# Gate logits from normalized tokens and head outputs, in a perceiver layer with routed experts

## The chip, the core and the metric

The kernel runs on one core of a Trainium2 chip. The metric is device time in microseconds (us); the time before is the median of three runs. In the text PE is TensorE (matrix multiplication), DVE is VectorE, ACT is ScalarE, POOL is GpSimd and SP is SyncE, which here only issues transfers. One execution of the kernel was profiled, and every row that is shown comes from it unless another kernel is named. "Granted clock" is the share of full speed that PE's clock was given.

## What is computed

There are 32 sequences of 32 tokens, 512 wide, so 1024 tokens or eight tiles of 128. All numbers are float32. Three steps follow each other, each added to its input:

```
x = x + cross_attention(layernorm(x), context)    # context: 32 x 257 x 384
x = x + self_attention(layernorm(x))              # 16 heads of 32, rotary q and k
x = x + experts(layernorm(x))

def experts(xf):                                  # 8 experts, hidden 1024
    scores = sigmoid(xf @ gate_w.T + balance_bias)
    top2 = the two best experts of each token, shares normalized to 1
    h = silu(xf @ w1[e].T)
    return sum over the two: share * (h @ w2[e].T)
```

The change bears on the gate, `xf @ gate_w.T`. Its argument is the normalized sum of what went into self attention, x, and of what came out of it: `out @ Wo.T + bo`, where `out` holds the heads' outputs.

## The kernel before

The eight token tiles are treated as four pairs, numbered 0 to 3 (`p`); tile 2p + i is tile i of the pair. Cross attention runs first (in groups `g` of four sequences), and its last groups already hold the first steps of pair 0. Then comes a loop over pairs 0 to 2, written out by hand: it attends for pair p and prepares pair p+1 meanwhile. Pair 3 is written out after the loop, mixed with the first work of the experts. A scheduler sets each engine's order from this text, with fixed queues: an instruction that waits holds back all behind it on its engine.

The steps, with their names in the code and the PSUM or SBUF names that the profile shows:

- `norm` (and `normalized`, `rstd_of`, L180) normalizes a pair for self attention into y: statistics on DVE, the power -1/2 on POOL (rs, L185), scaling on ACT. `turn` transposes y into yT on PE (spt), with one copy on ACT and one on DVE (syT). `project` (pp, L380) makes q and k in halves, `rotate` (L396 to L409) turns them on DVE, `values` (ppv, L818) makes v.
- `scores` (pqs, L833) multiplies q and k of all heads in pieces of 32 by 32. It writes a PSUM tile of which there is one only, shared with `attend` (pos, L875). DVE takes the maximum and subtracts it (smx L841, sex L843), ACT makes the exponential (L849). `shares` sums, divides and transposes on DVE (ssm, src, sex, aT). `attend` multiplies with v, and DVE adds the value bias (oT, L882).
- `finish` multiplies oT by the output matrix (ppo, L894), adds the result to x on DVE (L898), and writes x out. `norm2` takes statistics of the new x and scales it (fy, L915).
- The gate comes one pair later. `gate_turn` transposes the raw x of a tile on PE (fpt, L931), ACT copies it (fyT, L933), and `gate_logits` multiplies it by the centred gate weights gwc (pg, L940), four multiplications with only 8 columns each. DVE scales with rs and adds the bias (lg, L944). Since gwc has its mean over the 512 inputs removed, the mean of x needs no subtraction.
- `pick` (L955 to L999) finds the two best experts and their shares by some 25 small DVE operations and an exponential on ACT (a sigmoid in the last pair). `places` (pr, L1010 to L1032) counts the rows ahead, and POOL scatters the rows with four indirect DMAs into lists in memory (xs_d), one list for each expert. These lists were filled with zeros by eight DMAs (`fill`, L169), which SP issues after the attention weights.
- `order` (L1053 to L1116) counts after pair 2, ranks the experts, and lets SP load the first weights (w1), the first two blocks of rows of the biggest expert (xse) and w2. `early_turn` (xpe), `early_hidden` (phe, L1148) and `early_out` (poe, L1162) compute this expert's early rows. All other rows follow in the expert stage.

PSUM tiles named ps rotate through four buffers. A column group is a multiplication with 32 stationary columns that writes 32 of the 128 partitions; four can stand side by side. The kernel already uses such groups in `xquery` (pbt, L467) and `xmix` (pc, L599).

The large room `ewp` (three buffers of 16 KB in each partition) serves context tiles, then pair 0's data (`rooms[0]`, `rooms[1]`), then expert weights.

## Time and profile before

| | |
|---|---|
| median of three runs | 565.48 us (563.83 to 568.45) |
| the profiled execution's own time | 566.19 us |
| its span in the trace | 564.5 us |
| mean granted PE clock | 0.975 |
| PE busy | 525.1 us, 93% of the span, 4716 records |
| PE weight loads busy | 340.8 us, 60% |
| DVE busy | 254.0 us, 45% |
| ACT busy | 123.2 us, 22% |
| POOL busy | 83.5 us, 15% |
| self attention, roughly | 140 to 302 us of the span |

The busy shares say how much of the span an engine had something in work. They do not say what a stage waits for. For that one reads the chain that ended last (for each piece: start, length, what), the timeline of an engine (start, length, engine, line, operation, output and inputs, shape, count, and in brackets the idle time before it and what ended it), and windows (busy time of each engine in a stretch, with the granted clock). A float32 multiplication appears as two records, a transpose as one.

### The profile page before, as it was taken

Reading aid. Unit: us, or ns where it says so; the run is one execution under the profiler, and the core shown is the slowest. Engines: PE = TensorE matmul, PEld = TensorE weight load, DVE = VectorE, ACT = ScalarE, POOL = GpSimd, SP = SyncE. Lnnn points to the kernel's source line nnn. Section 1 sums busy time; section 2 is a strip of 40 time slices with the busy share of each in tenths; the row PEclk is TensorE's granted clock in tenths of the full one; section 3 lists DMA queues with packets and bytes.
Section 4 is the critical chain, followed back from the end, with each engine's and each line's share of the span. In section 5 each row is a group of like instructions: output and inputs, shape, how many; then the busy total and the mean of one; then the engine's idle time right before and its main releaser. Section 6 shows DMA issues by size and latency. Waiting matters only on the chain.

```text
span 564.5 us, 11301 instructions
## 1 busy us (share of the span) xinstructions
PE 525.1 (93%) x4716; PEld 340.8 (60%) x4716; DVE 254.0 (45%) x758; ACT 123.2 (22%) x274; POOL 83.5 (15%) x120
## 2 busy tenths in 40 slices
PE   6999797999999999998969999999999999999992
PEld 3646354566584875776548456547657475768580
DVE  6657778747567765668534032203122121222220
ACT  3534444323313312212022021002011010102010
POOL 2110221110001012021302110122120202112211
PEclk9999999999999999798989999999999999999997
DMA  8999979999910002012295341657553554746421
GB/s 281 383 372 395 318 244 324 357 387 386 384 58 38 3 24 93 2 42 76 81 381 216 90 100 69 238 133 221 167 168 111 128 198 154 215 159 197 161 27 21
DMA packets 43086, 104.51 MB, mean 185 GB/s; under 512 B 3985, under 2 KB 7185, under 8 KB 42002
## 3 DMA queue, kind: packets, MB, share of 16 engines
q1 hardware_dynamic: 38434, 94.91, 46.8%
q0 software_dynamic: 4592, 8.78, 7.7%
q8 instruction: 39, 0.64, 0.5%
q14 instruction: 21, 0.17, 0.1%
HBM read 75.50 MB, written 28.18 MB: 184 GB/s over the span
## 4 chain that ended last, share of the span: by engine, by line
PE 69%; DVE 2%; issue 1%; ACT 1%; POOL 0%; POOLq 0%; ACTq 0%
PE ph L1344 18%; PE fpo L1397 15%; PE pp L380 8%; PE ppv L818 5%; PE ppo L894 4%; PE fpq L1311 4%; PE phe L1148 3%; PE poe L1162 2%; PE pg L940 2%; PE pos L875 2%; PE pqs L833 2%; PE phb L1365 1%; PE xpt L1326 1%; ACT xT L176 1%; PE fpt L931 1%
## 5 line engine op out<-in xcount | busy, mean ns | idle before, releaser
L1344 PE MATMUL ph<-xT,w 128*128 128x288 f32 (+4 forms) x448 | 100.2, 382 | 3.1 <-ACT xT L176 3.1
L1344 PEld LDWEIGHTS ph<-xT,w 128*128 128x128 f32 x448 | 79.0, 190 | 19.6 <-ACT xT L176 3.7
L1397 PE MATMUL fpo<-w,hT 128*128 128x512 f32 x192 | 84.4, 596 | 0.0
L1397 PEld LDWEIGHTS fpo<-w,hT 128*128 128x128 f32 x192 | 35.9, 190 | 43.9 <-issue 43.7
L1350 DVE TENSOR_TENSOR hT<-ph,sg 128x288 f32<-128x288 f32 (+4 forms) x56 | 23.6, 422 | 61.7 <-ACT sg L1349 61.7
L1402 DVE TENSOR_SCALAR fob<-fpo,share 128x512 f32<-128x512 f32 x12 | 9.0, 751 | 77.0 <-PE fpo L1397 77.0
L1349 ACT ACTIVATE sg<-ph 128x288 f32<-128x288 f32 (+4 forms) x56 | 21.5, 383 | 85.0 <-PE ph L1344 83.5
L505 DVE BATCH_NORM_STATS2 st<-n 128x6 f32<-128x384 f32 x64 | 32.7, 549 | 2.1 <-DMA n<-in_ctx_dram 2.1
L194 POOL DMA_INDIRECT out_dram<-fob,idx x12 | 18.5, 1542 | 93.7 <-DVE fob L1402 80.9
L176 ACT COPY xT<-xpt 128x512 f32<-128x512 f32 (+2 forms) x12 | 6.0, 496 | 112.5 <-PE xpt L1326 112.4
L894 PE MATMUL ppo<-ao,oT 128*128 128x512 f32 x64 | 30.1, 624 | 0.0
L194 POOL DMA_INDIRECT out_dram<-fob,plc x9 | 13.9, 1541 | 101.5 <-DVE fob L1316 84.9
L519 POOL TENSOR_TENSOR rs<-v,mhalf 128x9 f32<-128x9 f32 x8 | 14.4, 1798 | 80.7 <-DVE v L517 42.6
L380 PE MATMUL pp<-syT,aq 128*128 128x256 f32 x96 | 25.7, 427 | 0.0
L633 PE MATMUL po<-wvo,uT 128*128 128x512 f32 x48 | 22.4, 602 | 1.2 <-ACT uT L626 1.2
L818 PE MATMUL ppv<-av,syT 128*128 128x512 f32 x48 | 23.3, 635 | 0.0
L475 PE MATMUL pq<-x1T,mq 128*128 128x256 f32 x96 | 23.1, 385 | 0.0
L1311 PE MATMUL fpq<-w,hT 128*32 128x128 f32 (+1 forms) x576 | 22.3, 309 | 0.0
L380 PE MATMUL pp<-syT,ak 128*128 128x256 f32 x96 | 22.3, 385 | 0.0
L1032 POOL DMA_INDIRECT xs_d<-fy,pi x16 | 17.0, 1064 | 35.3 <-DVE pi L1028 21.9
L380 PEld LDWEIGHTS pp<-syT,aq 128*128 128x128 f32 x96 | 20.2, 216 | 3.3
L894 PEld LDWEIGHTS ppo<-ao,oT 128*128 128x128 f32 x64 | 12.6, 199 | 14.2 <-issue 14.0
(269 smaller groups left out, 732.5 us busy)
## 6 DMA issues: line engine op xcount, KB each, us to landing
xs_d<-zero SPq DMA_DIRECT2D x8, 2112.0 KB, 20.5
w<-in_w1T_dram SPq DMA_DIRECT2D x16, 1024.0 KB, 8.4
w<-in_w2T_dram SPq DMA_DIRECT2D x16, 1024.0 KB, 8.2
nT<-in_ctxT_dram SPq DMA_DIRECT2D x8, 1542.0 KB, 9.6
n<-in_ctx_dram SPq DMA_DIRECT2D x32, 384.0 KB, 7.0
xs<-xs_d SPq DMA_DIRECT2D x4, 528.0 KB, 9.3
x_sb<-in_x_dram SPq DMA_DIRECT2D x8, 256.0 KB, 6.7
out_dram<-x_sb SPq DMA_DIRECT2D x8, 256.0 KB, 2.0
```

What stands on the lines that cost most here:

```text
L194: nc.gpsimd.indirect_dma_start(out=dst, out_offset=bass.IndirectOffsetOnAxis(ap=place, axis=0), in_=ob, in_offset=None, bounds_check=n * ( ...
L380: nc.tensor.matmul(pp[:, i, :], w[:, k, ts(e, P)], yT[:, k, :], start=(k == 0), stop=(k == KD - 1),)
L475: nc.tensor.matmul(pq[:, 0 : 2 * P], mq[:, k, ts(c, P)], x1T[:, k, :], start=(k == 0), stop=(k == KD - 1),)
L505: nc.vector.bn_stats(st[:, r, :], n[:, r // 2, r % 2, :] if r < 8 else nl)
L633: nc.tensor.matmul(po, uT[:, c, :], wvo[:, c, :], start=(c == 0), stop=(c == KC - 1))
L818: nc.tensor.matmul(pp, st[p]["yT"][:, k, ts(i, P)], av[:, k, :], start=(k == 0), stop=(k == KD - 1),)
L894: nc.tensor.matmul(pp, st[p]["oT", i][:, k].rearrange("p b q -> p (b q)"), ao[:, k, :], start=(k == 0), stop=(k == KD - 1),)
L1311: nc.tensor.matmul(po[ts(g, Q), 0:w], hT[:, f, ts(h, Q)], w2[:, f, ts(j, w)], start=(f == 0), stop=(f == KF - 1),)
L1344: nc.tensor.matmul(ph[:, 0:n], w1[:, k, ts(f, P)], t["xT"][:, k, 0:n], start=(k == 0), stop=(k == KD - 1),)
L1349: nc.scalar.activation(sg[:, 0:n], ph[:, 0:n], AF.Sigmoid)
L1350: nc.vector.tensor_mul(hT[:, f, 0:n], ph[:, 0:n], sg[:, 0:n])
L1397: nc.tensor.matmul(po, hT[:, f, ts(c, P)], w2[:, f, :], start=(f == 0), stop=(f == KF - 1),)
```

## The change

Four things are changed together.

1. **The gate's logits are put together from two parts.** For the part of x before self attention, `gate_tokens` multiplies gwc with yT, the already transposed normalized tokens (pgy, four column groups, both tiles at once). `gate_scaled` adds the four groups by a multiplication with the matrix `summed` (pgt) and ACT multiplies by the standard deviation std that the normalization had divided by (ga). For the part from self attention, `gate_heads` multiplies oT with gwo, the product of the output matrix and the gate weights (pgh, column groups), and `gate_logits` adds the groups (pg) and both parts (DVE, then rs and bias as before). The transposes of x (fpt, fyT) are gone.
2. **gwo is made once in the kernel.** `gate_fold` multiplies gwc with the output matrix (pgf) and with its bias (pgb), `gate_fold2` adds groups and transposes (pgo). This needs the output matrix in its other orientation, so it is loaded a second time (o2, 1 MB), into the second half of `rooms[1]`, and the eight zero fills are issued behind this load. gwc is padded with zeros from 8 to 32 columns.
3. **Logits and `pick` of pairs 0 and 1 stand in their own pair's turn**, after the next pair's `values`, and not in the next pair's turn behind the second scores.
4. **The last pair and its early rows are ordered anew**: `values` of both tiles stand among the scores, `order` comes ahead of `attend`, a one-column sigmoid loads ACT's table early, both copies of the early rows' transposes are on ACT, and both tiles' logits come ahead of `early_turn`.

The core of the diff:

```diff
+                std = spool.tile([P, 2], F32, tag="std", name="std")
+                nc.vector.tensor_tensor(std, ve, rs, ALU.mult)
...
-                        fill(aw["last"])
...
+                if g == NTT - 2:
+                    with tc.issue_after(aw["last"]):
+                        room(0, "sw0")
+                        aw["o2"] = load_weight(aWo, rooms[1][:, 2 * KD * N2 :])
+                    fill(aw["last"])
...
+            def gate_fold():
+                pm = ps.tile([P, D], F32, tag="ps", name="pgf")
+                for k in range(KD):
+                    nc.tensor.matmul(
+                        pm[ts(k, Q), :], gwc[:, k, :], aw["o2"][:, k, :],
+                        start=True, stop=True,
+                    )
+                gf = rooms[1][:, 2 * KD * N2 : 2 * KD * N2 + D]
+                nc.scalar.copy(gf, pm)
...
+            def gate_fold2(gf):
+                pm = ps.tile([P, D], F32, tag="ps", name="pgo")
+                for k in range(KD):
+                    nc.tensor.matmul(
+                        pm[:, ts(k, Q)], gf[:, ts(k, P)], summed, start=True, stop=True
+                    )
...
-            def gate_turn(p, i):
-                pt = ps.tile([P, KD, P], F32, tag="ps", name="fpt")
-                for k in range(KD):
-                    nc.tensor.transpose(pt[:, k, :], x_sb[:, t, ts(k, P)], ident)
-                xT = rt.tile([P, KD, P], F32, tag="fyT", name="fyT")
-                nc.scalar.copy(xT, pt)
...
+            def gate_tokens(p):
+                pg = ps.tile([P, D], F32, tag="ps", name="pgy")
+                for k in range(KD):
+                    nc.tensor.matmul(
+                        pg[ts(k, Q), 0:N2], gwc[:, k, :], st[p]["yT"][:, k, :],
+                        start=True, stop=True,
+                    )
...
+            def gate_heads(p, tiles=(0, 1)):
+                for j, i in enumerate(tiles):
+                    oT = st[p]["oT", i]
+                    for k in range(KD):
+                        nc.tensor.matmul(
+                            pg[ts(k, Q), ts(j, P)], gwo[:, k, :],
+                            oT[:, k].rearrange("p b q -> p (b q)"),
+                            start=True, stop=True,
+                        )
...
-                    evac(c, xT[:, :, ts(c, P)], pt)
+                    nc.scalar.copy(xT[:, :, ts(c, P)], pt)
...
+            gf = gate_fold()
+            gate_tokens(0)
             for p in range(NP - 1):
                 scores(p, 0)
+                gate_tokens(p + 1)
+                if p == 0:
+                    gate_scaled(0)
+                    gate_fold2(gf)
                 project(p + 1, 0, 0)
                 shares(p, 0)
                 scores(p, 1)
-                if p:
-                    gate(p - 1, 0)
-                    gate(p - 1, 1)
-                    pick(p - 1)
+                gate_scaled(p + 1)
...
+                gate_heads(p)
                 finish(p, 0)
                 norm2(p, 0)
                 finish(p, 1)
                 norm2(p, 1)
                 if p < NP - 2:
                     values(p + 1)
+                    gate_logits(p)
+                    pick(p)
                     step(turn, p + 2)
             p = NP - 1
             scores(p, 0)
-            gate_turn(p - 1, 0)
-            gate_turn(p - 1, 1)
-            scores(p, 1)
-            gate_logits(p - 1, 0)
-            gate_logits(p - 1, 1)
+            values(p, (0,))
+            gate_logits(p - 1)
+            last = scores(p, 1)
             pick(p - 1)
-            values(p, (0,))
             shares(p, 0)
+            values(p, (1,))
+            with tc.issue_after(last.ins), tc.issue_after(st[p - 1]["en"]):
+                table = keep.tile([P, 1], F32, name="table")
+                nc.scalar.activation(table, mhalf[:, 0:1], AF.Sigmoid)
             places(p - 1)
+            order()
             attend(p, 0)
-            values(p, (1,))
-            order()
             shares(p, 1)
+            gate_heads(p, (0,))
             finish(p, 0)
-            norm2(p, 0)
-            attend(p, 1)
-            gate(p, 0)
+            with tc.issue_after(attend(p, 1).ins):
+                norm2(p, 0)
+            gate_heads(p, (1,))
             finish(p, 1)
             norm2(p, 1)
+            gate_logits(p)
             early_turn()
-            gate_turn(p, 1)
             early_hidden(0)
-            gate_logits(p, 1)
             pick(p)
```

More of the change, by code (lines that the diff above doesn't have):

```diff
@@ L43 @@
 ASCALE = HD ** -0.5
-G1, B1, BQ, BK, BV, AQ, AK, AV, NCOL = 0, 4, 8, 12, 16, 20, 24, 28, 44
+G1, B1, BQ, BK, BV, AQ, AK, AV, AO, NCOL = 0, 4, 8, 12, 16, 20, 24, 28, 32, 44
 RBO, RAO, RBB, NROW = 0, 512, 1024, 1032
@@ L69, in tile_perceiver_layer @@
     aWoT: bass.AP,
+    aWo: bass.AP,
     gateT: bass.AP,
@@ L185, in rstd_of @@
         nc.gpsimd.tensor_tensor(rs, ve, mhalf[:, :n], ALU.pow)
-        return rs
+        return rs, ve
     def stats_of(src, mv):
@@ L337, in normalized @@
                     stats_of(x_sb[:, 2 * p + i, :], mv[:, i, :])
-                rs = rstd_of(mv, 2)
+                rs, ve = rstd_of(mv, 2)
+                std = spool.tile([P, 2], F32, tag="std", name="std")
+                nc.vector.tensor_tensor(std, ve, rs, ALU.mult)
+                st[p]["std"] = std
                 nb = spool.tile([P, 2], F32, tag="nb", name="nb")
@@ L805, in tile_perceiver_layer @@
             nc.vector.tensor_scalar_mul(gm, pm[:, 0:NE], -1.0 / D)
-            gwc = keep.tile([P, KD, NE], F32, name="gwc")
+            gwc = rt.tile([P, KD, Q], F32, tag="gwc", bufs=1, name="gwc")
+            nc.gpsimd.memset(gwc, 0.0)
             nc.vector.tensor_tensor(
-                gwc, gw, gm.unsqueeze(1).to_broadcast([P, KD, NE]), ALU.add
+                gwc[:, :, 0:NE], gw, gm.unsqueeze(1).to_broadcast([P, KD, NE]), ALU.add
             )
+            summed = copies[:, 0, 0, :]
+            gwo = rt.tile([P, KD, Q], F32, tag="gwo", bufs=1, name="gwo")
+            bg = rt.tile([P, 1], F32, tag="bg", bufs=1, name="bg")
+            def gate_fold():
[7 more added lines that the diff above has]
+                nc.scalar.copy(gf, pm)
+                pm = ps.tile([P, D], F32, tag="ps", name="pgb")
+                for k in range(KD):
+                    nc.tensor.matmul(
+                        pm[ts(k, Q), 0:1], gwc[:, k, :], col[:, AO + k : AO + k + 1],
+                        start=True, stop=True,
+                    )
+                nc.scalar.copy(bg, pm[:, 0:1])
+                return gf
+            def gate_fold2(gf):
[4 more added lines that the diff above has]
+                    )
+                nc.scalar.copy(
+                    gwo, pm[:, 0 : KD * Q].rearrange("p (k q) -> p k q", q=Q)
+                )
             scatters = []
@@ L848, in scores @@
                 )
-                nc.scalar.activation(ex, ex, AF.Exp, scale=ASCALE)
                 st[p]["ex", i] = ex
+                return nc.scalar.activation(ex, ex, AF.Exp, scale=ASCALE)
             def shares(p, i):
@@ L881, in attend @@
                 oT = wk.tile([P, KD, 4, T], F32, tag="oT", bufs=3, name="oT")
-                nc.vector.tensor_tensor(
+                added = nc.vector.tensor_tensor(
                     oT.rearrange("p k b q -> p b k q"),
@@ L888, in attend @@
                 st[p]["oT", i] = oT
+                return added
             def finish(p, i):
@@ L909, in norm2 @@
                 stats_of(x_sb[:, t, :], mv[:, 0, :])
-                rs = rstd_of(mv, 1)
+                rs, _ = rstd_of(mv, 1)
                 nb = spool.tile([P, 1], F32, tag="nb1", name="nb")
@@ L920, in norm2 @@
                 st[p]["rs", i] = rs
-            def gate(p, i):
-                gate_turn(p, i)
-                gate_logits(p, i)
-            def gate_turn(p, i):
-                t = 2 * p + i
-                pt = ps.tile([P, KD, P], F32, tag="ps", name="fpt")
-                for k in range(KD):
-                    nc.tensor.transpose(pt[:, k, :], x_sb[:, t, ts(k, P)], ident)
-                xT = rt.tile([P, KD, P], F32, tag="fyT", name="fyT")
-                nc.scalar.copy(xT, pt)
-                st[p]["gT", i] = xT
@@ L936, in gate_logits @@
-            def gate_logits(p, i):
-                xT = st[p]["gT", i]
-                pg = ps.tile([P, D], F32, tag="ps", name="pg")
+            def gate_tokens(p):
+                pg = ps.tile([P, D], F32, tag="ps", name="pgy")
                 for k in range(KD):
                     nc.tensor.matmul(
-                        pg[:, 0:NE], xT[:, k, :], gwc[:, k, :],
-                        start=(k == 0), stop=(k == KD - 1),
-                    )
-                nc.vector.scalar_tensor_tensor(
-                    st[p]["lg"][:, i, :], pg[:, 0:NE], st[p]["rs", i], bb,
-                    op0=ALU.mult, op1=ALU.add,
-                )
+                        pg[ts(k, Q), 0:N2], gwc[:, k, :], st[p]["yT"][:, k, :],
+                        start=True, stop=True,
+                    )
+                gy = rt.tile([P, N2], F32, tag="gy", name="gy")
+                nc.scalar.copy(gy, pg[:, 0:N2])
+                st[p]["gy"] = gy
@@ new lines, in gate_scaled @@
+            def gate_scaled(p):
+                pg = ps.tile([P, D], F32, tag="ps", name="pgt")
+                for i in range(2):
+                    nc.tensor.matmul(
+                        pg[:, ts(i, NE)], st[p]["gy"][:, ts(i, P)], summed[:, 0:NE],
+                        start=True, stop=True,
+                    )
+                ga = rt.tile([P, 2, NE], F32, tag="ga", name="ga")
+                for i in range(2):
+                    nc.scalar.activation(
+                        ga[:, i, :], pg[:, ts(i, NE)], AF.Identity,
+                        scale=st[p]["std"][:, i : i + 1],
+                    )
+                st[p]["ga"] = ga
@@ new lines, in gate_heads @@
+            def gate_heads(p, tiles=(0, 1)):
+                if "go" not in st[p]:
+                    st[p]["go"] = rt.tile([P, 2, P], F32, tag="go", name="go")
+                n = len(tiles)
+                pg = ps.tile([P, D], F32, tag="ps", name="pgh")
+                for j, i in enumerate(tiles):
+                    oT = st[p]["oT", i]
+                    for k in range(KD):
+                        nc.tensor.matmul(
+                            pg[ts(k, Q), ts(j, P)], gwo[:, k, :],
+                            oT[:, k].rearrange("p b q -> p (b q)"),
+                            start=True, stop=True,
+                        )
+                nc.scalar.activation(
+                    st[p]["go"][:, tiles[0] : tiles[0] + n, :],
+                    pg[:, 0 : n * P].rearrange("p (i q) -> p i q", q=P),
+                    AF.Identity, bias=bg,
+                )
@@ new lines, in gate_logits @@
+            def gate_logits(p, tiles=(0, 1)):
+                pg = ps.tile([P, D], F32, tag="ps", name="pg")
+                for i in tiles:
+                    nc.tensor.matmul(
+                        pg[:, ts(i, NE)], st[p]["go"][:, i, :], summed[:, 0:NE],
+                        start=True, stop=True,
+                    )
+                for i in tiles:
+                    lg = st[p]["lg"][:, i, :]
+                    nc.vector.tensor_tensor(
+                        lg, pg[:, ts(i, NE)], st[p]["ga"][:, i, :], ALU.add
+                    )
+                    nc.vector.scalar_tensor_tensor(
+                        lg, lg, st[p]["rs", i], bb, op0=ALU.mult, op1=ALU.add
+                    )
@@ L983, in pick @@
                     en = rt.tile([P, 2, 2], F32, tag="en", name="en")
-                    nc.scalar.activation(en, top[:, :, 0:2], AF.Exp, scale=-1.0)
+                    st[p]["en"] = nc.scalar.activation(
+                        en, top[:, :, 0:2], AF.Exp, scale=-1.0
+                    ).ins
                     nc.vector.tensor_scalar_add(en, en, 1.0)
@@ L1522 @@
                     "xattn_ln1_g", "xattn_ln1_b", "xattn_bq", "xattn_bk", "xattn_bv",
-                    "attn_bq", "attn_bk", "attn_bv",
+                    "attn_bq", "attn_bk", "attn_bv", "attn_bo",
                 )
             ]
-            + [np.zeros((P, NCOL - 32), np.float32)],
+            + [np.zeros((P, NCOL - 36), np.float32)],
             axis=1,
@@ L1543 @@
         "aWoT": a["L0_attn_Wo"].T,
+        "aWo": a["L0_attn_Wo"],
         "gateT": a["L0_ffn_gate_w"].T,
```

## Prediction

> **What bounds the kernel now.** I read the 40 slices of the page first, then the chain that ended last through the attention stage, then windows of that stage cut at the clock's own steps. The slices say that TensorE (PE) is busy nearly everywhere, and that its granted clock drops only between 226 and 296 us, in the attention pairs.

> ```profile
> span 564.5 us, 11301 instructions
> ...
> PE   6999797999999999998969999999999999999992
> ...
> PEclk9999999999999999798989999999999999999997
> ```

> The chain shows what PE does there. In pair 2, after the second scores (pqs), it turns a tile of tokens (fpt), waits for ACT to copy the result (fyT), and multiplies it with the gate (pg):

> ```profile
> 185.24 3.65 PE pp L380 x16
> ...
> 230.24 0.60 PE fpt L931 x4
> ...
> 230.92 0.59 ACT fyT L933
> ...
> 231.55 1.06 PE pg L940 x8
> 232.61 0.86 PE fpt L931 x4
> 233.48 0.82 PE pos L875 x45
> 234.30 1.81 PE pg L940 x8
> 236.10 5.25 PE pp L380 x16
> ```

> The reader is to see that the same pg costs 1.06 and then 1.81, and the same 16 projections 3.65 and then 5.25. The windows say why (columns: window, PE, weight loads, DVE, ACT, POOL, granted clock, DMA share, GB/s):

> ```profile
> 191.63:195.04 3.41, 3.41 (x87) 3.08 (x87) 1.75 (x9) 1.19 (x2) 0.00 (x0) 1.00 0.02 5
> 195.04:198.45 3.41, 3.41 (x10) 2.69 (x9) 3.09 (x18) 0.20 (x1) 0.40 (x2) 0.50 0.00 0
> 229.15:232.56 3.41, 2.68 (x141) 2.39 (x115) 2.18 (x4) 2.02 (x4) 0.00 (x0) 1.00 0.02 5
> 232.56:235.98 3.42, 3.42 (x78) 3.01 (x77) 1.41 (x6) 0.58 (x1) 0.00 (x0) 0.50 0.02 5
> 235.98:239.39 3.41, 3.41 (x9) 2.78 (x10) 3.11 (x18) 0.20 (x1) 0.40 (x2) 0.50 0.00 0
> ```

> The clock falls to half for whole windows of 3.41 us, each after one filled with small multiplications. This happens in four places: one window in pair 1, two in pair 2, two from 263.3, one from 287.2. That is 6 x 3.41 x 0.5 = 10.2 us. So the attention stage is bound by PE, and its gate costs more than its instructions.

> **Prices.** A multiplication is two records in the trace. Those that write 32 partitions each run four at a time:

> ```profile
> 92.09 1.47 PE L599 MATMUL pc<-n,eT 128*32 128x384 f32 x16
> 99.31 0.64 PE L467 MATMUL pbt<-x1T,mq 128*32 128x256 f32 x8
> ```

> Eight records of 391 ns in 0.64; net of the neighbours' overlap pbt takes 0.57 (99.31 to 99.88). pgy has exactly this shape: 0.57. pgh for two tiles is half as wide and twice as many: 0.57 (0.3 for one). pgf, 8 records 512 wide, from pc: 1.47 x (8x512)/(16x384) = 0.98. The sums over copies (pgt, pg) are 4 records of old pg's kind, which took 1.06 for 8: 0.53. pgo is 8 such: 1.06. pgb has no near row for one column in 32-wide groups; pb (4 full-array records, 0.36 net) is above it and zero below: I take 0.2.

> **Pair 0: +5.0.** Added: pgf 0.98, pgb 0.2, pgy twice 1.14, pgt twice 1.06, pgo 1.06, pgh 0.57. ACT's copies lie beside scores. The wait of 1.25 at 153.86, which no engine releases, could be covered: -1.25 at best; I leave it.

> **Pair 1: -3.3.** Removed: 190.11 to 194.66 less 0.68 for pos = 3.87, and the slow projections 5.24 - 3.65 = 1.59; together 5.46. Added: pg 0.53, pgy 0.57, pgt 0.53, pgh 0.57 = 2.2.

> **Pair 2, up to ppo: -5.0.** Removed: 230.24 to 236.10 less pos 0.82 = 5.04, and 1.60; added pg, pgy, pgt 1.63.

> **DVE: +0.6.** pick now stands ahead of the syT copy's end and the next softmax. About eleven small operations (0.1 to 0.2 each) delay syT to some 2.2 us after pg, while PE reaches pgy after 2.1 to 1.7: I take 0.45 and 0.15. The rest of pick is hidden under pp (3.65).

> **The clock rule.** [...] The longest PE idle here is 2.28 us (before 285.25), and 191.63 to 195.04 has none, yet half clock followed. [...] I go by the trace: windows with under about 1.2 us of wide work fall. The new stretch pg, spt, pqs, pgy has 1.4 us of it besides scores and should stay fast. The fold in pair 0 may not: up to +1.7, kept for the range.

> **Last pair: -6.6.** Its order is laid out on before's time axis from 250.84, where ppo began. pgh 0.57 and ppo bring PE to 258.4, pqs to 259.6, and values (3.55) now fill the wait of 2.0 before 262.12; pg ends at 263.7. DVE reaches the end of the first sex at 263.0 instead of 262.07, for nb of tile 4 now stands before x_sb of tile 5, and waits for POOL's rs (0.57). Second pqs ends at 264.9, values at 268.45, pr and pn at 269.2, pos at 270.6. But DVE: first softmax to 265.4, gate and pick with aT 267.9, second smx and sex 269.3, rest of pick 270.7, ssm and src 271.6, then places, sex, aT to 273.4, pi 273.55, order's first two, oT 274.6. PE waits for it from 270.6: a **new wait of 4.05**, and probably half clock after it (1.45). Tile 6's ppo ends at 280.0, pos 281.2, oT (behind x_sb) 281.9, pgh 0.3, tile 7's ppo 285.8 against 291.54; pg 286.3.

> Now the early rows. POOL and SP decide:

> ```profile
> 275.38 1.06 POOL L1032 DMA_INDIRECT xs_d<-fy,pi  x1 [5.18 <-DVE oT L882]
> ...
> 280.87 1.01 SPq L208 DMA_DIRECT2D w<-in_w1T_dram  x2
> 282.26 0.37 SPq L1104 DMA_DIRECT2D xse<-xs_d  x1
> ```

> The rows landed at 291.3, 9.0 after issue, behind 2 MB of w1. pi comes 1.0 earlier, so xse issues at 281.3; eidi (279.5) comes at 275.5, so w1 goes 4.0 earlier and about 1 MB of it is over, at 390 GB/s 2.7 us less: landing about 287.5 (286.3, where PE is ready, to 289). xpe and two copies on ACT, 1.65: phe starts at 289.15 against 295.02, and pg (0.79) no longer cuts into phe: -6.6 with rounding.

> **Hidden.** The second output matrix is 1 MB on SP's queue, before the eight zero fills: 2.7 us at 385 GB/s. It should land about 117 and is needed at 148.5; the fills end near 160 and the first scatter is at 208.5, so 48 us cover them. If the load waited for its room (used by a context tile before), pgf would wait with it; the built order shows no such wait on that DMA. If the cover of the fills were gone, scatters would come 2.7 us later. POOL's memset of gwc and four std on DVE have 6 us before pgf. ACT's table load (1.28 at 295.65) held nobody and moves before v's copy, which has 8 us (1.28 if that were gone). The last scatter, rows and weights move with phe. The expert stage is left as it is.

> **Sum.** 5.0 - 3.3 - 5.0 + 0.6 - 6.6 = -9.3. Against the profiled execution's own 566.19 that is 556.9; the median of the runs shown lies 0.7 lower: 556.2. A measurement of this kernel can tell about 1% from no change.

> **Rivals.** (1) Half clock stays: other small windows take the place of the gate's. Against it, pp follows every pair of small pieces; for it, pair 0's fold has 4 us of them. Price 1.7 + 3.2 + 1.7 = 6.6: 562.8. (2) The last pair brings nothing, since xse lands at 291 as before or oT comes later: for it, scatters start only 1.0 earlier; against it, w1 is out of the way 4 us sooner. 562.8. (3) The column groups do not run together: then pgf, four pgy and four pgh cost four times their width, +2.9, +4.6 and about +5: **568.7, slower than before**. It decides from 2.8 times the price. pbt and pc speak against it; new weights per group are in both. [...] (4) The change does not move the end: 566. This would need a wait behind phe that does not move with it, such as rows of the other experts; their read was issued at 310.6 and used at 325.5, which leaves room.

> **Numbers.** Forecast 0.6, half clock 0.12, last pair nothing 0.12, column groups 0.06, no effect 0.04, something unnamed and slower 0.06. The forecast's own range: pair 0 between 3.7 and 6.7, loop -8.3 to -7, DVE 0 to 1.5, last pair -9 to -3.5, that is 551.5 to 563. With the rivals I go to 567. Faster by over 1% means under 559.8: the forecast and a little of the others, 0.64. Slower means over 571.1: column groups with half clock, or the unnamed, 0.12. Within: 0.24.

> **What would show it.** fpt and fyT gone; pgy at 0.6 per four; granted clock 1.00 between 188 and 258 but for a possible window at pair 0; pair 1 and 2 each 36.7 us from ppo to ppo; PE waiting about 4 us for oT before tile 6's pgh; xse landing 5 us before the end of its old time; phe 15 us long. I am wrong if pgy takes 1.5 or more, if pgf waits for the load, or if xpe starts later than 288 on the new trace's own axis (the sum puts it at 287.5 - 2.7 = 284.8).

## The result, and the profile after

The changed kernel takes 569.27 us (median, 564.34 to 572.11) against 567.16 (563.16 to 568.55) for the kernel before on the same chip: ratio **1.0055**, 95% interval 1.0038 to 1.0073. So it is about half a percent slower. The forecast was 556.2, 1.6% faster, with a range of 551 to 567. The profiled span is 567.1 against 564.5.

The page of the changed kernel, in the slices that are shown of before; the last line is the DMA queue that carries instructions:

```profile
span 567.1 us, 11444 instructions
...
PE   6999798999979989999859999999999999999991
...
PEclk9999999999979999999878999999999999999997
...
q8 instruction: 39, 0.64, 0.5%
```

The clock's drops have moved: none is left between 226 and 255 us; a new one stands in the twelfth slice (156 to 170 us), which is pair 0, and the last pair has three low slices (8, 7 and 8, from 269 to 312) where it had two (8 and 8). The chain through pair 2 (start, duration, engine and tile) is what was forecast:

```profile
231.40 0.34 PE pg L1018 x4
231.75 0.93 PE spt L369 x8
232.68 1.22 PE pqs L875 x72
233.89 0.57 PE pgy L972 x8
234.46 3.65 PE pp L384 x16
...
239.87 3.56 PE pp L384 x16
```

fpt and fyT are gone, pgy costs 0.57, and the projections behind the second scores take 3.56 where they took 5.25. The same view through pairs 0 and 1 holds the first surprise:

```profile
147.82 0.98 PE pgf L828 x6
...
148.85 0.46 PE pgy L972 x8
...
151.64 0.91 PE pgo L846 x8
...
156.08 1.20 PE pqs L875 x71
157.28 3.31 issue
160.59 0.21 PE pqs L875
160.80 0.89 PE pgt L983 x4
161.69 6.57 PE pp L384 x16
...
200.37 1.71 issue
```

PE stands still for 3.31 us inside one run of 32x32 multiplications, of which 127 of 128 records are done. No engine releases it. The kernel before has such a wait in the same scores, a shorter one, after 43 records (PE's timeline of before):

```profile
155.11 0.93 PE L833 MATMUL pqs<-pair 32*32 32x32 f32 x85 [1.25 <-issue]
```

In the changed kernel the clock is at half after the wait (columns as in the windows shown of before):

```profile
147.50:157.28 9.78, 9.78 (x318) 7.34 (x316) 4.42 (x7) 3.92 (x12) 0.00 (x0) 1.00 1.06 382
157.28:160.59 3.31, 0.00 (x1) 0.00 (x0) 0.00 (x0) 0.00 (x0) 0.00 (x0) 1.00 0.58 210
160.59:163.90 3.31, 3.31 (x11) 2.82 (x12) 2.29 (x4) 1.05 (x3) 0.00 (x0) 0.54 0.02 6
163.90:168.00 4.10, 4.10 (x12) 3.15 (x10) 1.43 (x3) 0.00 (x0) 0.00 (x0) 0.54 0.00 0
```

The second surprise is in the last pair, in its chain:

```profile
278.85 0.98 POOL xs_d L1116
...
280.13 8.99 DMA xs_d<-fy,pi
...
289.32 3.83 DMA xse<-xs_d
...
293.20 1.98 PE xpe L1214 x8
```

and on SP's queue (start, time to the last issue, line):

```profile
278.34 1.01 SPq L209 DMA_DIRECT2D w<-in_w1T_dram  x2
289.32 0.37 SPq L1188 DMA_DIRECT2D xse<-xs_d  x1
```

The last scatter of pair 2 needs 8.99 us to land; w1's 2 MB were issued 1.79 ahead of it (278.34 against 280.13). Before, w1 came 1.6 after it (280.87 against 279.30), and xse was issued 3.0 after the last scatter; the scatter's line on POOL's timeline of before is

```profile
279.30 0.97 POOL L1032 DMA_INDIRECT xs_d<-fy,pi  x1 [0.30 <-issue]
```

xse now waits for the scatters (w2, behind it on SP's queue, goes out at 289.96, before at 282.82) and PE waits 4.59 for xse, though it was through with tile 7 at 288.6, some 1.0 earlier than forecast when both are counted from the last ppo of two tiles.

By stretches, from the end of the turns (spt) of pair 0, between starts of ppo, and from the last ppo of two tiles to the start of poe:

| us | before | after | forecast | measured |
|---|---|---|---|---|
| pair 0 | 20.76 | 30.68 | +5.0 | +9.9 |
| pair 1, its DVE term in it | 40.12 | 38.90 | -2.85 | -1.2 |
| pair 2, its DVE term in it | 41.46 | 36.71 | -4.85 | -4.75 |
| last pair | 59.86 | 58.96 | -6.6 | -0.9 |
| start of pair 0, expert stage | | | 0 | -0.5 |

The measured column adds up to +2.6, the difference of the spans. Two stretches carry the miss: 4.9 in pair 0 and 5.7 in the last pair; 1.6 more is in pair 1.

### The profile page after: what moved, and what is told of

It reads as the page before. It is cut to its first block, busy times and chain, and to the rows that moved or that the text cites. A ratio compares the mean times of both kernels' runs of the same rounds, so it can differ in the third digit from the quotient of the medians.

```text
span 567.1 us, 11444 instructions
## 1 busy us (share of the span) xinstructions
PE 523.0 (92%) x4772; PEld 336.2 (59%) x4772; DVE 254.2 (45%) x769; ACT 125.3 (22%) x288; POOL 83.1 (15%) x121
## 4 chain that ended last, share of the span: by engine, by line
PE 65%; issue 3%; DVE 2%; DMA 2%; POOL 1%; ACT 1%; POOLq 0%; SPq 0%; DVEq 0%
PE ph L1435 18%; PE fpo L1488 15%; PE pp L384 8%; PE fpq L1402 4%; PE ppv L860 4%; PE phe L1232 3%; PE ppo L937 2%; PE poe L1246 2%; DMA xs_d<-fy,pi 2%; PE pqs L875 1%; PE pos L917 1%; PE phb L1456 1%; PE xpt L1417 1%; POOL xs_d L1116 1%; DMA xse<-xs_d 1%
## 5 line engine op out<-in xcount | busy, mean ns | idle before, releaser
L860 PE MATMUL ppv<-av,syT 128*128 128x512 f32 x48 | 21.6, 596 | 1.1 <-issue 1.1
```

What stands on the lines that cost most here:

```text
L860: nc.tensor.matmul(pp, st[p]["yT"][:, k, ts(i, P)], av[:, k, :], start=(k == 0), stop=(k == KD - 1),)
```

## The experiments

**Theory A**: PE runs out of instructions. They come in blocks of 16 KB (0.64 MB in 39 packets on q8); by the theory a dense run of small multiplications uses up a block faster than the next one comes, so PE waits at the block's edge, where one block ends and the next begins; and the next one comes later still while the zero fills keep the DMA engines busy. **Theory B**, its rival: the wait belongs to data or to the fold itself. **Theory C**: the last pair's gain is lost because w1 goes ahead of the last scatters. **Theory D**, its rival: it is lost to DVE, the new wait for oT.

Counting PE's instructions in program order (four for a multiplication, being two loads and two multiplications in the trace, two for a transpose, one for a wait) puts the 3.31 in pair 0 and the 1.71 in pair 1 at places 256 apart or a multiple of it, with 127 of 128 records of pqs done in the one and 117 in the other. The order of PE's records in the trace (multiplications, weight loads and semaphore instructions) agrees: 2242 and 3522 stand ahead of them, and the difference of 1280 is five times 256. So the first experiment moves the places.

### a_pad: 128 more PE instructions

```
+            pad = psq.tile([P, 4, KD, P], F32, tag="pq", name="pad")
+            for j in range(32):
+                nc.tensor.matmul(pad[...], st[0]["qk", 0][...], st[0]["qk", 1][...], start=True, stop=True)
             gf = gate_fold()
```

> The changed kernel with 32 extra 32x32 multiplications (128 weight loads and matmuls in the trace's count, about 0.6 us, results unused) ahead of the fold of pair 0; nothing else. Theory A (instruction supply): PE's waits named issue, 3.31 in pair 0 and 1.71 in pair 1, come where the end of a 16 KB block of 256 instructions falls at the end of a run of small multiplications, so the next block is not there yet. The pad moves the ends by 128 instructions into the middle: both waits fall to under 0.5 (pair 0 perhaps to 1.3, as before, since the zero fills still move), the slow projections after the first (6.57) go back to 3.65, and the kernel gains 5 to 8.5 us: about 561 to 564. Rival B: the waits belong to the new small multiplications beside the scores (their copies on ACT[...]). Then they stay, and the kernel is 0.6 us longer.

Measured: 568.03 us, ratio to before 1.0041 (1.0027 to 1.0055). Pair 1 lost its waits and took 36.79. Pair 0's wait went to the first scores, with 99 of 128 records done, on PE's timeline:

```profile
155.53 0.40 PE L875 MATMUL pqs<-pair 32*32 32x32 f32 x29 [3.55 <-issue]
```

The shift is what the count says: the wait in the second pqs stood 254 instructions in, and the block edge now stands 199 into the first (two per record: 99.5). A wait that follows the count of instructions and not the data speaks for A. The time was a miss: 561 to 564 was expected, but the edge moved into another run of small work. The fold behind the wait then ran at half clock (pgo 1.75, pp 5.02), and xse was late as before, so the time hardly moved.

### a_rows: the rows' read ahead of w1

```
-                tail["w1"] = {0: expert_w1(e)}
                 xs = wk.tile([P, 2, YW], F32, tag="y", name="xse")
                 nc.sync.dma_start(xs, ...)
+                tail["w1"] = {0: expert_w1(e)}
```

> The changed kernel with the read of the first expert's early rows (xse) issued before the loads of its first weights (w1) instead of after them; nothing else. Theory C (collision): pair 2's scatters landed 9.0 us after the last issue instead of about 3, because w1's 2 MB were moving by then. With the read first, SP holds w1 until the scatters are through: they land by 283, xse by 287.5 (293.15), w1 by about 291, and phe starts at 290 to 291.5 instead of 295.8: 4 to 6 us less, about 564. Rival D: the scatters are slow by themselves or by the zero lists and x writes: xse lands at 292 or later as before, and w1 comes after it, so the kernel is 2 to 5 us longer.

Measured: 561.79 us, ratio **0.9931** (0.99 to 0.9962). Its chain:

```profile
280.88 2.74 DMA xs_d<-fy,pi
...
283.81 0.42 SPq L1187
...
285.02 8.73 DMA w<-in_w1T_dram
```

With w1 held back the scatter lands in 2.74 instead of 8.99. xpe follows tile 7 without a wait (289.20), and the last pair takes 51.56 instead of 58.96: theory C. What is left is that phe now waits for w1, whose second half lands at 293.75.

### a_pad_rows: both

> Both edits of the two kernels before. Theories A and C: the gains add, and the waits named issue in the last pair (1.10 and 0.87) go too, which now count: 554 to 559, ratio to before 0.975 to 0.988. If only one of the two theories holds, 561 to 565. If neither, 570 to 575.

Measured: 561.47 us, ratio 0.9925 (0.9895 to 0.9956). Last pair 52.20, pair 1 36.78, pair 0 still 31.29 with a wait of 3.42. By the bands of the expectation the time says that only one of the two theories holds. The stretches say why: the padding freed pair 1, but in pair 0 it had only moved the wait. Tile 6's pgh now shows the forecast's wait for oT, 3.15 (forecast 4.05), on PE's timeline:

```profile
275.97 0.66 PE L1004 MATMUL pgh<-oT,gwo 128*32 128x128 f32 x8 [3.15 <-DVE oT L924]
```

It doesn't hold the end: the last pair is still 7.7 below before. That speaks against D.

### b_pad: the kernel before, with 25 tiny multiplications ahead of the scores of pair 0

> The kernel before with 25 of the same extra multiplications (100 instructions, 0.5 us) ahead of pair 0's scores, so that a block of instructions ends at 242 of the 256 instructions of the second scores of pair 0 instead of at 86. Theory A: the wait there grows from 1.25 to about 3.3, PE falls to half clock behind it (2 to 3 us), and the kernel is 4 to 6 us longer, ratio about 1.008, without any change to its gate. Rival B: only the 0.5 us show.

Measured: 570.49 us, ratio 1.0077 (1.0043 to 1.0111). A wait of 2.49 appeared with half clock behind it (seven records of pp take 2.51, the seven ahead of the wait 1.71), and pair 0 grew from 20.76 to 25.30, though the 25 multiplications themselves take about 0.6 (64 records of the other padding took 0.75). So a few instructions of no use cost the kernel before some 4 us. The place was a miss: the block edge fell 15 instructions into pp, right after the first scores, and not into the second scores (PE's timeline):

```profile
156.77 2.51 PE L380 MATMUL pp<-syT,aq 128*128 128x256 f32 x7 [2.49 <-issue]
```

### a_short_rows: the fills cut short

This is a_rows with 384 of the 1024 rows of each list filled. The other rows stay unfilled, so it does less work than the kernels so far; a version that fills all of them comes below.

```
-                    xs_d[ts(e, LIST), :]...         zero...to_broadcast([P, LIST // P, YW])
+                    xs_d[e * LIST : e * LIST + 3 * P, :]...  zero...to_broadcast([P, 3, YW])
```

> The changed kernel with the rows of the experts read ahead of the loads of w1 (as in a_rows, 561.8 us) and with only the first 384 of the 1024 rows of each list filled with zeros, so that the eight fills end some 27 us earlier (near 133 instead of 160); the other rows of the lists are left unfilled. Theory A (PE waits for its instructions, and waits longer while the fills hold the DMA engines): the wait of 3.36 in the second scores of pair 0 shrinks to what pair 1 shows without fills, 1.4 to 1.7; no half clock follows, so pp of pair 0 takes 3.7 to 4.5 instead of 6.4; pair 1's wait of 1.4 stays where it is. Together 3 to 5 us less than a_rows: 557 to 559. Theory B (the wait belongs to the fold's own data, or to PE's queue, whatever the DMA does): the wait stays at 3.3 and the time at 561 to 562.

Measured: 556.44 us (four runs), ratio **0.9836** (0.9793 to 0.988). The chain at the place where PE had stood still:

```profile
152.59 0.91 PE pgo L846 x8
153.50 3.54 PE pp L384 x16
157.04 1.22 PE pqs L875 x72
...
158.80 3.56 PE pp L384 x16
```

The same instructions at the same places, with no wait and no half clock. Pair 0 takes 23.81 instead of 30.66. Theory B is out. A had the cause, and put the remaining wait too high (1.4 to 1.7 expected, none found). Pair 1 keeps its wait of 1.16, where no fill moves in either kernel (DMA share 0.00 during the 1.71 of the changed kernel, 0.58 during its 3.31).

The trace also tells when the block came. Two lines of the DMA view of the changed kernel from 156 to 162 us show the busy tenths of the 16 DMA engines in 40 slices, and the queue's one packet of instructions.

```profile
DMA  9999999999999998656544433211000000000000
...
q8 instruction: 1, 0.02, 1.1%
```

The packets of instructions begin 4.9 and 10.2 us after pgf starts with all rows filled (152.75 and 158.0), and 2.5 and 6.2 after it with 384 (151.25 and 155.0); these are starts of windows 0.25 wide, so each can lie up to 0.25 later. The fetch itself takes some 1.1 in both. PE resumes at 160.59, some 1.3 after the late one has ended.

This is so wherever PE stands still in this way. From 140 us to the end of the early rows, the fourteen profiles (the two kernels and the twelve experiments) have 28 waits of more than 0.3 us named issue inside a run of PE's work. In the count of instructions all 28 stand at the same place of the 256, to within one (in PE's records 1986 stand ahead of the 1.25 of before, and 2242, 3522, 6081 and 6338 ahead of the four waits of the changed kernel: each 193 or 194 past a multiple of 256), and in each of them PE resumes 1.3 to 1.6 us after a packet on q8 has ended. The waits named issue at the start of phe (2.0 to 2.6, in before, b_pad, b_short and a_gates) have neither sign and are another kind.

### a_short_pad_rows

> As a_short_rows, with the 32 tiny multiplications ahead of the fold that move every later instruction by 128 places (a_pad_rows, 561.5 us, waited 3.42 in the first scores of pair 0 and then ran the fold at half clock: 1.75 for pgo, 5.15 for pp). Theory A: the wait in the first scores shrinks to 1.4 to 1.7, the fold runs at full clock (pgo 1.0, pp 3.7), pair 1 has no wait, and the time falls by 3.5 to 5.5 to 556 to 558. Theory B: 561 to 562, wait 3.4 as before.

Measured: 556.05 us (four runs), ratio 0.9818 (0.9775 to 0.9862). There is a wait of 0.92 in the first scores, the fold is at full clock (pgo 0.91, pp 3.54), and pair 1 has no waits (36.81). Against a_short_rows the padding changes nothing that these intervals can tell.

### a_late_pad_rows: every row filled, but later

This is a_pad_rows with the fills behind the second softmax of pair 0.

```
-                    fill(aw["last"])
...
                 scores(p, 1)
+                if p == 0:
+                    ex = st[0]["ex", 1][:, 0, 0:16]
+                    late = nc.gpsimd.tensor_tensor(zero[:, 0:16], ex, ex, ALU.subtract)
+                    fill(late.ins)
```

> The changed kernel with rows first and the 32 tiny multiplications, all rows filled, but the fills start only after the second softmax of pair 0 (about 163 instead of 117) and move until about 206. Theory A: pair 0 has no long wait (1.4 to 1.7 in its first scores, pgo near 1.0, pp 3.7), as in a_short_pad_rows; pair 1 has its block edges away from its small multiplications and waits little although the fills now move beside it; the first scatter, near 207, lands up to a few us later and holds nobody. 556 to 559. Theory B: the wait of 3.4 stays in pair 0, 561 to 562. If the fills themselves slow PE or the loads of pair 1 in another way, pair 1 becomes 1 to 3 us longer and the gain is gone.

Measured: 564.95 us, ratio 0.9982 (0.996 to 1.0003). A miss in the sum and telling in the mechanism: the waits went where the fills went. The first scores of pair 0 wait 0.82, ahead of the fills. Then 2.10 at 169.53 in pos of pair 0, with half clock behind it (pp 5.34), and 2.10 at 200.30 in the second pqs of pair 1, with half clock again (pp 5.24). Pair 1 takes 40.94 where it took 36.8 without fills beside it. The first is 26 records into its run, the second 53; the count of instructions puts the block edges at 26.5 and 53.

### b_order: the kernel before, with order() ahead of the attention

```
             places(p - 1)
+            order()
             attend(p, 0)
             values(p, (1,))
-            order()
```

> The kernel before with one step moved in its last pair: the order of the experts (and with it the issue of w1) stands ahead of the first attention of the pair, as the change has it; its gate is the old one. Theory C (w1's 2 MB, issued ahead of the last scatters, hold these up, and so the read of the rows): w1 is issued ahead of the last scatter, the scatters land 6 to 9 after the last issue instead of about 3, xse is issued at 285 to 288 instead of 282.3, but then lands in about 4 instead of 9, so xpe starts within 2 of its old time (291.4), and the whole stays within 2 us of before (565 to 569). Theory D (the last pair of the changed kernel lost its gain by its own wait for oT, not by the transfers): the read of the rows moves earlier with w1, landing near 288, and the time is 1 to 3 us less than before.

Measured: 564.32 us, ratio 0.9984 (0.9957 to 1.0011): no difference. In the chain:

```profile
278.43 8.53 DMA xs_d<-fy,pi
...
287.16 3.62 DMA xse<-xs_d
```

This is the changed kernel's collision in the kernel before: w1 at 277.08, the last scatter takes 8.53 instead of 2.8, and xse goes out at 287.16 instead of 282.26. It lands within 1 us of its old time, 3.62 after its issue where it took 9.0 with w1 just ahead of it, and the last pair takes 59.74 for 59.86. Earlier weights bought no earlier rows: theory C, and the step of the forecast that failed.

### a_gates: the new gate with the old order of the last pair

```
-            values(p, (0,))
             gate_logits(p - 1)
...
-            order()
             attend(p, 0)
+            values(p, (1,))
+            order()
```

> The new gate alone: pairs 0 to 2 as the change has them, but the last pair in the order of before (values of tile 7 and the order of the experts after the first attention, norm2 before the second attention, the gate's logits after the early rows), and no separate load of ACT's table. Theory C: order() after the attention puts w1 behind the last scatters again, which land within 4 of the last issue, and xse is issued within 3 of it; pair 0 loses 9 to 10 and pairs 1 and 2 bring 6.5 as in the changed kernel; the last pair loses its two fpt turns (about 2). 565 to 568. If the late rows of the changed kernel come from its wait for oT and not from w1, xse lands as late here as there and the time is 568 to 571.

Measured: 565.69 us, ratio 0.9988 (0.9967 to 1.0008). The waits for instructions stand where they do in the changed kernel (127 records done in pair 0, 11 left in pair 1), on PE's timeline:

```profile
162.21 0.26 PE L875 MATMUL pqs<-pair 32*32 32x32 f32 x1 [3.86 <-issue]
203.62 0.28 PE L875 MATMUL pqs<-sqk,sqk 32*32 32x32 f32 x11 [1.70 <-issue]
```

and its DMA view from 270 to 300 us (KB each, median us to landing) shows the order of before:

```profile
xse<-xs_d SPq DMA_DIRECT2D x1, 528.0 KB, 8.8
xs_d<-fy,pi POOLq DMA_INDIRECT x4, 3.0
```

So the late scatters come with the new place of order() and not with the gate. Its last pair takes 55.41, 3.6 less than with the new order. The new gate alone is worth nothing here: pair 0's loss eats what pairs 1 and 2 and the last pair bring.

### b_short and b_short_rows: the same edits in the kernel before

> The kernel before with 384 of 1024 rows of each list filled, nothing else changed: what the fills cost the kernel before. Theory A: its one wait of 1.25 to 1.35 in pair 0 shrinks to 1.0 or goes, 564 to 566. If the fills slow other things too (loads, scatters), 560 to 563.

> The kernel before with both edits that freed the changed one: the rows of the experts read ahead of w1, and 384 of 1024 rows of each list filled, the rest left unfilled. Theory A+C (the change costs what it was priced at, and lost its gain to the two collisions, which the kernel before does not have): before gains at most its own wait of 1.25 in pair 0, and the rows land before tile 7 is done (291.5), where xpe started before (291.4), so nothing there: 563.5 to 566, while the changed kernel with the same edits is at 556.4. The change alone is then worth 7 to 10. Theory E (the two edits are simply good by themselves, in any kernel): before falls as far as the changed kernel did, to 553 to 557.

Measured: 565.55 us, ratio 1.0 (0.9985 to 1.0014), and 564.14, ratio 0.9966 (0.9949 to 0.9982). In b_short pair 0 loses its wait (19.30 instead of 20.76), and the time doesn't move by as much as these runs can tell; pairs 1 and 2 of its profile take 41.61 and 38.55, where before has 40.12 and 41.46. That the old gate's half-clock windows fall in one pair or the other is inferred from these four times. With rows first as well it is 0.3%. The same two edits bring the changed kernel from 569 to 556.4. By themselves they are worth little: they take away two collisions that the change had run into. With both gone from both kernels the change is worth 1.0 - 0.9836/0.9966 = 1.3%, some 7.4 us (from two separate ratios, so without an interval of its own).

### a_split_pad_rows: a version with every row filled

This is a_pad_rows with the fills in two parts.

```
-    def fill(ins):
+    def fill(ins, a=0, b=5):
+                xs_d[e * LIST + a * P : e * LIST + b * P, :] ... to_broadcast([P, b - a, YW])
...
+                if p == 0:
+                    oz = st[0]["oT", 0].rearrange("p k b q -> p (k b q)")[:, 0:16]
+                    late = nc.gpsimd.tensor_tensor(zero[:, 0:16], oz, oz, ALU.subtract)
+                    fill(late.ins, 5, LIST // P)
                 gate_heads(p)
```

> A version with every row filled: the changed kernel with rows first and the 32 tiny multiplications, where the fills of rows 0 to 639 of each list stay at their place (10.8 MB, done near 145) and those of rows 640 to 1023 (6.5 MB, some 17 us) start when the heads' output of pair 0 is there (about 175) and end near 192. Theory A: no fill moves beside the small multiplications of pair 0 (150 to 157) or of pair 1 (190 to 205), so the waits for instructions are as short as with 384 rows (0.9 in pair 0, none in pair 1), and the time is that of a_short_pad_rows, 555.5 to 557.5. If instead the sum of the bytes counts and not their place, 561.

Measured: 556.75 us (556.29 to 557.91), ratio **0.9843** (0.9807 to 0.9879), better than both kernels. Five eighths of the rows are filled ahead of pair 0, the rest between its scores and those of pair 1. PE's timeline at pair 0:

```profile
151.20 1.04 PE L875 MATMUL pqs<-pair 32*32 32x32 f32 x99
152.96 0.35 PE L875 MATMUL pqs<-pair 32*32 32x32 f32 x29 [0.72 <-issue]
...
154.27 1.06 PE L846 MATMUL pgo<-copies,pair 128*128 128x32 f32 x8
155.16 3.70 PE L384 MATMUL pp<-syT,aq 128*128 128x256 f32 x16
```

The block edge is at record 99 again, as in a_pad. There the wait was 3.55, and half clock followed; here it is 0.72, and pp takes 3.70. By stretches against before: pair 0 +5.3, pair 1 -3.4, pair 2 -4.75, last pair -7.2, start +0.6; together -9.45 at poe, where the forecast had -9.3. That these two are so near is in part luck: this kernel has two edits that the forecast didn't have, the padding, which is 0.75 us of work, and the rows ahead of w1, which bring the last pair of the kernel before 1.4 as well (58.40 in b_short_rows, 59.75 in b_short). This version without the padding was not tried.

## Why the prediction was wrong

- **New operations: right.** pgf 0.98 (0.98), pgb 0.05 (0.2), pgy 0.46 to 0.57 (0.57), pgt 0.54 (0.53), pgo 0.91 (1.06), pgh 0.57. The column groups run together (eight records of pgy, 0.38 each, in 0.57), so rival 3 is out. Between a_short_rows and b_short pair 0 differs by 4.5; the sum said 5.0.
- **Pair 0: the step that failed is "The wait of 1.25 at 153.86, which no engine releases, could be covered: -1.25 at best; I leave it."** It was taken for a wait that the change could only shorten. By what the experiments show it was PE waiting for its instructions, and the change put hundreds of small instructions ahead of the next such place, while the fills moved. The sum of what was found: 4.5 for the new operations, 2.06 more wait (3.31 for 1.25), 3.0 of half clock in the pp behind it (6.57 against 3.56 in a_short_rows) and 0.35 in pgt (0.89 for 0.54), together the 9.9. The half clock of the fold that the range allowed for (+1.7) came from this wait, not from the small work.
- **Pair 1: right in size, spoilt by the same step.** -1.2 for -2.85; where the padding moves the block edge it is -3.3 (36.79).
- **DVE's term, +0.6: not seen.** pgy follows the first scores at once in both pairs (194.99 and 233.89). Without it the sum had -3.3 for pair 1, which the padded kernels show, and -5.0 for pair 2.
- **Pair 2: right**, -4.75 for -4.85.
- **The clock: right behind the gate, but the limit that was read is not shown.** From 168 to 276 us the changed kernel has full clock, as forecast; rival 1 is out for pairs 1 and 2. That limit, about 1.2 us of wide work in a window (counted here as full-array work of 128 columns or more), fits the trace that it was read from: at most 1.2 in the windows ahead of one at half clock, at least 1.3 in all others from 144 us to the early rows. In the changed kernel it fails: the windows from 147.18 and from 198.38 had 0.6 and 0.9 us of it, and no drop followed. The drop in pair 0 stands behind the wait. In pairs 0 to 2, over all kernels, waits for instructions of 2.1 to 3.9 were followed by half clock and those of 0.4 to 1.7 were not; in the last pair of the changed kernel two waits of 0.87 and 0.86, with 0.3 of work between them, were (0.50 from 276.9 to 280.3).
- **"Hidden", the fills: wrong.** They were priced for when they end ("the fills end near 160") against the first scatter at 208.5. What they do to the fetch of instructions until then was left out (the packet ahead of the wait begins 10.2 us after pgf with all rows filled, 6.2 with 384). The second output matrix itself held nobody: pgf starts at 147.82, right behind spt.
- **Last pair: the step that failed is "w1 goes 4.0 earlier and about 1 MB of it is over ... landing about 287.5".** w1 went earlier, but not xse: the sum moved one transfer and forgot that the last scatters, which xse has to await, would now stand behind it. On the axis of before (the last ppo of two tiles began 3.3 later) xse was issued at 286.0, not 281.3, and landed at 289.9, not 287.5; phe started at 292.6, not 289.15, and ran partly at half clock after PE's stop (0.50 up to 300, 0.90 from 300 to 304), 17.2 long instead of 14.9 (the 15.7 of before less pg's 0.79): 3.4 and 2.3 are the 5.7 that are missing. xpe started at 293.20 on its own axis, past the 288 that the prediction had set as a sign of being wrong. Tile 7's end was right to within 1.0: with the rows ahead of w1 the stretch shrinks by 8.3, of which 1.4 is what the same edit brings the kernel before. So rival 2 (the last pair brings nothing, since the rows come late) was right on this stretch; its 562.8 left pair 0 out.
- **The wait for oT: right in kind**, 3.15 where the instruction waits are gone, for 4.05. In the changed kernel 0.86 of it is left behind two waits for instructions (1.10 and 0.87), and the wait for xse comes after all of them.

## What to carry to other kernels

A wait in the chain that no engine releases, in a run of small instructions or just behind one, can be a cost with a place: here instructions added ahead of it moved it (a_pad) or made it grow (2.49 in b_pad for 1.25), and bulk transfers beside it made it longer (3.31 in the changed kernel, none at that place in a_short_rows). Look whether a packet of instructions ends just before the engine resumes, and count instructions between two such waits. When a load is issued earlier, list every transfer that is still to be issued on any queue before the one that you wait for; here the last scatter behind 2 MB of weights took 8.5 to 9.0 us to land, where it took 2.7 to 2.8 ahead of them. When a sum is made of stretches, write each stretch's end as a time and check the transfers against each, so that a miss shows in which stretch it sits.
